# Q, K, V and router logits by token from one product per tile, turned by VectorE and transposed back, in a new written order

## The chip, the cores and the metric

The kernel runs on one core of a Trainium2 chip. The metric is the device time of one execution in microseconds (us). The core's engines work side by side, each through its own list of instructions in order: TensorE (matmuls, in the profile PE, its weight loads PEld), VectorE (DVE), ScalarE (ACT), GpSimd (POOL), and SyncE (SP), which issues most transfers. They wait for one another through semaphores.

## The reference, cut to what matters

`x` has 16 items of 256 tokens with 128 numbers each, all float32. An attention layer with 16 heads of 8 numbers, then a layer of eight experts of which each token uses two; each layer is added to its input and normalized.

```python
qkv = (x @ w_qkv).reshape(B, S, 3, heads, head_dim)
Q, K, V = qkv[:, :, 0], qkv[:, :, 1], qkv[:, :, 2]
Q, K = apply_rope(Q), apply_rope(K)      # x * cos + concat([-x2, x1]) * sin, halves of 4 numbers
attn = einsum('bqhd,bkhd->bhqk', Q, K) * head_dim ** -0.5
attn = softmax(where(causal, attn, NEG_INF))
x = layernorm(x + einsum('bhqk,bkhd->bqhd', attn, V).reshape(B, S, dim) @ w_proj + b_proj)
logits = flat_x @ W_router + b_router    # the two largest choose the experts and weigh them
out = layernorm(x + sum over the two chosen e of w_e * (relu(x @ W1[e] + b1[e]) @ W2[e] + b2[e]))
```

## The kernel before

`main_path` registers its work as some 1,550 small operations in a plan: each has an engine, a function that issues its instructions, and the operations that it waits for. `Plan.order` then issues them in one list, `ORDER`, written out by hand as the numbers under which they were registered. On each engine the instructions run in the order of that list. Costs and ranks given to `op` don't enter in the version that runs; only `ORDER` does.

`attention(b)` handles one item of 256 tokens. Two transposes (L780) turn `x` so that its 128 numbers lie along the partitions, and ScalarE copies the result to `xT` (L783). For Q and then K, `project` (L793) makes two products of 128 x 256: with the weights `wqk_sb`, and with `wsw_sb`, the same weights with the halves of each head exchanged (four copies at the start, L651). `turn_parts` multiplies these by the cosine and sine tables in `rope_sb` (L802, L803), and a sum gives the turned Q or K with the head's numbers along the partitions, in `qk` (L810). ScalarE makes four copies of Q, `qTm`, each with all heads but a quarter masked to zero (L822). V and the part of the router's logits that depends on `x` come from a third product by token (`project_v`, L838, 136 columns for each half of the tokens); `place_v` copies V into the padded `va` and the logits next to `x` (L847, L851).

Scores are made in three rounds (L871), each into the one buffer `sc`; ScalarE takes the exponential (L896), and GpSimd sets to zero what the causal mask forbids (L881). `weigh` (L912) multiplies with V. The sums of the exponentials go through memory and come back spread over partitions; VectorE multiplies by their inverse (L956), `project_o` (L966) makes the attention's result, and VectorE adds `x`, takes the moments and normalizes (L978 to L996).

Tokens of four, four and two items, and then of six, are routed (`route`): VectorE computes logits (L1077 to L1080), chooses (L1067 to L1090) and counts places, and GpSimd scatters the rows into memory (L1140). An expert block reads up to 256 such rows, and does the two layers (L1339, L1360) with ScalarE's bias and relu between them (L1352); GpSimd sends the rows back (L1387). The blocks of the first ten items follow the attention of the last ones in the list. At the end `combine` adds and normalizes; `keep_warm` gives TensorE a few products to do meanwhile (L1557).

The buffers named `m` are three buffers of TensorE's result memory, shared by transposes, projections, routing counts and blocks.

Of the kernel before, what the change touches and what calls it, by code (L numbers as in the profile page):

```python
# [11 lines left out]
F32 = mybir.dt.float32  # L12
# [299 lines left out]
7 0 45 46 1 14 47 9 15 12 2 11 50 29 81 6 3 4 22 10 13 48 49 5 82 51 52 24 56 54 53 86 17 21 19  # L312
23 87 30 57 93 55 59 94 16 58 88 18 60 20 25 83 121 65 31 61 26 157 84 85 122 123 124 91 66 89
68 158 44 90 62 92 63 159 160 161 126 32 95 96 125 127 197 128 162 133 132 64 163 131 98 69 99
67 198 70 71 8 97 130 72 33 101 104 129 102 100 164 233 169 103 234 134 73 74 141 75 142 166
105 106 107 108 135 143 167 136 27 109 76 170 202 203 204 168 28 110 138 165 139 199 111 137
144 209 656 200 201 140 208 112 171 145 206 146 147 172 655 77 148 177 173 149 113 178 78 150
179 151 238 79 210 239 207 174 152 34 205 80 175 114 653 176 235 180 658 115 116 236 211 237
117 118 240 212 181 182 183 184 185 153 186 35 244 245 214 243 215 187 188 213 273 120 119 220
154 657 217 216 242 155 274 246 278 279 659 275 276 241 218 250 219 280 251 277 221 309 310 281  # L320
284 189 222 223 247 282 190 248 311 156 252 224 249 191 192 193 253 37 285 225 256 314 283 254
286 312 290 194 195 196 664 313 291 226 255 315 316 257 385 386 665 258 662 227 259 260 261 293
666 36 390 391 392 318 317 294 319 320 667 672 670 287 262 671 228 288 654 387 668 295 263 349
321 292 322 669 388 389 289 350 326 678 296 297 298 327 264 680 229 673 395 323 324 328 679 299
300 265 301 394 354 355 351 352 329 302 353 230 356 325 231 393 232 332 303 396 330 405 661 333
406 38 674 675 676 331 357 266 267 358 360 399 334 335 400 336 425 677 41 268 361 304 397 337
338 339 426 340 407 402 398 362 359 401 427 537 681 403 686 269 430 538 366 408 305 367 428 429
431 404 409 410 432 434 685 270 363 435 688 364 411 271 306 682 436 433 542 369 341 307 412 413
# [126 lines left out]
def main_path(  # L455
# [87 lines left out]
    def load_x(b):  # L543
# [5 lines left out]
        )  # L549

    load_x(0)
    qk_op = dma(
        -99.0, 128, lambda: load(wqk_sb, w_qkv[:, 0 : 2 * D].rearrange("d (s e) -> d s e", s=2))
    )
    rope_op = [
# [1119 lines left out]
```

## Time and profile before

Three runs took 426.84 us at the median, 424.04 and 431.35 at the ends. The profile is of one other execution, which took 373.53 us.

| | us |
|---|---|
| profiled execution | 373.53 |
| its span, first to last instruction | 372.1 |
| first exponential starts, last one starts | 12.7, 185.5 |
| TensorE busy with L793, L838 | 42.5, 10.4 |
| VectorE busy with L802, L803, L810 | 40.0 |
| ScalarE busy with L896, L822, L847 | 90.1, 29.6, 5.9 |

Busy times of matmuls overlap[...]: 128 instructions of L793 sum to 42.5 us, though the engine starts one every 0.215 us. So a matmul's price is read from the time until the next one can start, and busy time is used only to compare stages. "Idle before" in a group is time in which the engine had nothing to do just ahead of these instructions, with the instruction that ended it.

### The profile page before, as it was taken

Reading aid. Unit: us, or ns where it says so; the run is one execution under the profiler, and the core shown is the slowest. Engines: PE = TensorE matmul, PEld = TensorE weight load, DVE = VectorE, ACT = ScalarE, POOL = GpSimd, SP = SyncE. Lnnn points to the kernel's source line nnn. Section 1 sums busy time; section 2 is a strip of 40 time slices with the busy share of each in tenths; the row PEclk is TensorE's granted clock in tenths of the full one; section 3 lists DMA queues with packets and bytes.
Section 4 is the critical chain, followed back from the end, with each engine's and each line's share of the span. In section 5 each row is a group of like instructions: output and inputs, shape, how many; then the busy total and the mean of one; then the engine's idle time right before and its main releaser. Section 6 shows DMA issues by size and latency. Waiting matters only on the chain.

```text
span 372.1 us, 9773 instructions
## 1 busy us (share of the span) xinstructions
PE 332.6 (89%) x2960; PEld 246.6 (66%) x2960; DVE 202.6 (54%) x731; ACT 252.3 (68%) x547; POOL 218.0 (59%) x252
## 2 busy tenths in 40 slices
PE   5999999979999696797999887999999899989980
PEld 3554555545566353444589767999898899989960
DVE  3440566786368879854567872143321267635551
ACT  2889778878788665677655453666666489978642
POOL 5155343446887489488822567777777446553632
PEclk9999999999999999699999999899999999999997
DMA  4100354131321221165345436665765687776472
GB/s 127 44 3 13 113 75 118 32 102 62 118 63 55 74 59 40 31 154 171 87 114 152 132 93 170 162 187 155 218 196 156 178 249 237 231 204 194 142 213 76
DMA packets 53098, 46.51 MB, mean 125 GB/s; under 512 B 14610, under 2 KB 39577, under 8 KB 53042
## 3 DMA queue, kind: packets, MB, share of 16 engines
q1 hardware_dynamic: 48626, 37.36, 37.5%
q0 software_dynamic: 4416, 8.47, 6.8%
q8 instruction: 27, 0.44, 0.5%
q14 instruction: 29, 0.24, 0.2%
HBM read 33.53 MB, written 12.67 MB: 124 GB/s over the span
## 4 chain that ended last, share of the span: by engine, by line
PE 55%; DVE 16%; ACT 11%; DMA 6%; issue 5%; POOL 4%; ACTq 0%; DVEq 0%; POOLq 0%; SPq 0%
PE m L1339 14%; PE m L1360 13%; PE sc L871 8%; PE ps_o L912 7%; ACT pr L896 7%; PE m L793 4%; PE m L966 3%; POOL rows L1140 2%; DMA rows_in<-rows 2%; DVE lg L1079 2%; DVE x_sb L996 2%; POOL pr L881 2%; PE ps_o L1557 1%; DMA out_dram<-yout 1%; PE m L1323 1%
## 5 line engine op out<-in xcount | busy, mean ns | idle before, releaser
L896 ACT ACTIVATE pr<-sc 128x2048 f32<-128x2048 f32 x48 | 90.1, 1877 | 26.8 <-PE sc L871 24.9
L1387 POOL DMA_INDIRECT back<-y,rows_in x74 | 72.8, 984 | 57.0 <-ACT y L1379 33.8
L881 POOL TENSOR_SCALAR_AFFINE_SELECT pr<-pr 128x1024 f32<-128x1024 f32 (+1 forms) x48 | 67.3, 1412 | 58.8 <-ACT pr L896 58.5
L1352 ACT ACTIVATE hT<-m,b_sb 128x128 f32<-128x128 f32 (+1 forms) x224 | 71.7, 407 | 21.8 <-PE m L1339 19.1
L1140 POOL DMA_INDIRECT rows<-x_sb,dest x64 | 65.3, 1020 | 22.7 <-issue 17.0
L1360 PE MATMUL m<-w_sb,hT 128*128 x592 | 75.5, 277 | 2.0 <-issue 1.1
L1339 PE MATMUL m<-rT,w 128*128 128x128 f32 (+1 forms) x448 | 75.8, 315 | 1.0 <-DVE rT L1332 0.4
L1360 PEld LDWEIGHTS m<-w_sb,hT 128*128 128x128 f32 x592 | 70.9, 192 | 4.8 <-ACT hT L1352 1.7
L1339 PEld LDWEIGHTS m<-rT,w 128*128 128x128 f32 x448 | 63.0, 194 | 5.9 <-DVE rT L1332 1.1
L871 PE MATMUL sc<-qTm,qk 32*128 32x512 f32 x384 | 55.7, 650 | 6.6 <-ACT pr L896 5.0
L912 PE MATMUL ps_o<-pr,va 128*32 128x128 f32 (+1 forms) x1024 | 49.9, 334 | 2.5 <-POOL pr L881 2.4
L1379 ACT ACTIVATE y<-y,rows_in 128x128 f32<-128x128 f32 x74 | 27.7, 401 | 30.4 <-DVE y L1370 30.1
L912 PEld LDWEIGHTS ps_o<-pr,va 128*32 128x32 f32 x1024 | 28.3, 111 | 29.4 <-issue 12.9
L1370 DVE TENSOR_TENSOR y<-m,b_sb 128x128 f32<-128x128 f32 (+1 forms) x56 | 18.7, 334 | 51.1 <-PE m L1360 41.8
L822 ACT ACTIVATE qTm<-qk,rows_sb 128x256 f32<-128x256 f32 x64 | 29.6, 506 | 1.8 <-DVE qk L810 1.8
L871 PEld LDWEIGHTS sc<-qTm,qk 32*128 32x128 f32 x384 | 15.2, 185 | 19.3 <-ACT pr L896 12.2
L793 PE MATMUL m<-xT,wqk_sb 128*128 128x256 f32 x64 | 22.5, 436 | 0.9 <-ACT xT L783 0.9
L802 DVE TENSOR_TENSOR part<-m,rope_sb 128x256 f32<-128x256 f32 x32 | 13.1, 410 | 18.6 <-PE m L793 18.1
L966 PEld LDWEIGHTS m<-wproj_sb,o 128*128 128x128 f32 x128 | 16.1, 190 | 7.2 <-issue 1.9
L956 DVE TENSOR_TENSOR o<-o,spread 128x512 f32<-128x512 f32 x16 | 13.7, 853 | 12.2 <-DMA spread<-recs 12.2
L793 PE MATMUL m<-xT,wsw_sb 128*128 128x256 f32 x64 | 20.0, 395 | 0.0
L1332 DVE COPY rT<-m 128x128 f32<-128x128 f32 (+1 forms) x32 | 10.6, 340 | 16.1 <-PE m L1323 14.2
(152 smaller groups left out, 362.6 us busy)
## 6 DMA issues: line engine op xcount, KB each, us to landing
w<-in_L_ffn_W_dram SPq DMA_DIRECT2D x56, 256.0 KB
spread<-recs SPq DMA_DIRECT2D x16, 256.0 KB
ys<-back SPq DMA_DIRECT2D x16, 256.0 KB
rows_in<-rows SPq DMA_DIRECT2D x38, 65.0 KB
rows_in<-rows SPq DMA_DIRECT2D x18, 130.0 KB
x<-in_L_attn_x_dram SPq DMA_DIRECT2D x16, 128.0 KB
w_sb<-in_L_ffn_W_dram SPq DMA_DIRECT2D x8, 256.0 KB
out_dram<-yout SPq DMA_DIRECT2D x16, 128.0 KB
```

Of the source, the lines that this page charges most:

```text
L793: nc.tensor.matmul(ps.get()[:, c, :], w[:, s, :], xT.get(), start=True, stop=True)
L822: lambda j=j: nc.scalar.activation(qTm.get()[:, j, :], qk.get()[:, 0], AF.Copy, scale=rows_sb[:, j : j + 1]),
L871: nc.tensor.matmul(ps.get()[:, g], qk.get()[rg, 1, ts(kt, P)], qTm.get()[rg, js, kt * P : S], start=True, stop=True,)
L881: nc.gpsimd.affine_select(out=pr.get()[:, :, :, 0:P], in_=pr.get()[:, :, :, 0:P], compare_op=ALU.is_ge, fill=0.0, base=0, pattern=[[0, GRO ...
L896: lambda pr=pr, ps=ps: nc.scalar.activation(pr.get(), ps.get(), AF.Exp),
L912: nc.tensor.matmul(pso.get()[ts(g, 32), t, kt * P : S], va_t[:, kt, 2 * g + t].rearrange("p u c -> p (u c)")[:, 16 * u : 16 * u + 32], pr. ...
L1140: nc.gpsimd.indirect_dma_start(out=g.rows[:, :], out_offset=bass.IndirectOffsetOnAxis(ap=g.dest[:, k, t - g.t0 : t - g.t0 + 1], axis=0), i ...
L1339: nc.tensor.matmul(ps_h[i].get()[:, c, :], w.get()[:, ts(i * per + c, P)], rT.get()[:, 0 : n * P], start=True, stop=True,)
L1352: nc.scalar.activation(hT.get()[:, at, 0 : n * P], ps_h[i].get()[:, c, :], AF.Relu, bias=bias)
L1360: nc.tensor.matmul(ps_y.get()[:, i, :], hT.get()[:, c, i * P : (i + 1) * P], w2_sb[:, bass.ds(e, 1), c, :].rearrange("p o d -> p (o d)"), ...
L1379: nc.scalar.activation(y.get()[:, i, :], y.get()[:, i, :], AF.Copy, scale=rows_in.get()[:, i, D + 1 : DX],)
L1387: put = nc.gpsimd.indirect_dma_start(out=g.back[:, :], out_offset=bass.IndirectOffsetOnAxis(ap=rows_in.get()[:, i, D : D + 1].bitcast(I32) ...
```

## The change

Q, K, V and the logits of half an item's tokens (128) now come from one product: `xT` of these tokens against all 392 columns of `w_sb`, so that tokens lie along the partitions. VectorE turns Q and K there, with tables by token: two short products take each half of the heads times the sine into `side` (the halves exchanged by the way the operand is read), one product in place takes the cosine, and one sum writes `turned`. `place_v` copies V and the logits out of the same buffer, once per half of the tokens. Four transposes (`turn_heads`) put the heads back along the partitions, into one buffer `ps_t`: VectorE copies K out of it as `kT`, and ScalarE's four masks read Q from it directly. The scores then read `kT` and `qTm`.

The second set of weights with its copies and the two large tables are gone. 16 KB of the table are loaded (`waves`) and transposed once at the start; the scale of Q goes into the mask's factors. `keep_warm` takes another operand. `ORDER` is a new list throughout: the sequence of items, blocks and scatters in it differs too.

```diff
 ORDER = """
-7 0 45 46 1 14 47 9 15 12 2 11 50 29 81 6 3 4 22 10 13 48 49 5 82 51 52 24 56 54 53 86 17 21 19
...
+5 0 44 45 3 13 1 2 49 14 50 9 7 8 30 156 51 46 47 52 157 4 12 48 57 55 54 56 53 10 6 161 29 162
...
-    wqk_sb = const.tile([P, 2, D], F32, name="wqk_sb")
-    wvr_sb = const.tile([P, DR], F32, name="wvr_sb")
-    rope_sb = const.tile([P, 2, 2, S], F32, name="rope_sb")
+
+    w_sb = const.tile([P, 3 * D + E], F32, name="w_sb")
+    wr_sb = w_sb[:, 3 * D : 3 * D + E]
+
+    waves = const.tile([HD, 2, S], F32, name="waves")
+    turns_sb = const.tile([P, NT, 2, HD], F32, name="turns_sb")
...
-    qk_op = dma(
-        -99.0, 128, lambda: load(wqk_sb, w_qkv[:, 0 : 2 * D].rearrange("d (s e) -> d s e", s=2))
+    w_ops = [
+        dma(-99.0, 192, lambda: load(w_sb[:, 0 : 3 * D], w_qkv)),
+        dma(-96.0, 4, lambda: load(wr_sb, w_router)),
+    ]
+    waves_op = dma(
+        -98.0,
+        16,
+        lambda: load(waves, rope.rearrange("p (a c s) -> p a c s", a=2, c=2)[0:HD, 1]),
     )
-    rope_op = [
-        dma(
-            -98.0,
-            256,
-            lambda s=s: load(
-                rope_sb[:, :, s, :],
-                rope.rearrange("p (a c s) -> p a c s", a=2, c=2)[:, s],
-            ),
-        )
-        for s in range(2)
-    ]
     rows_op = dma(-97.0, 2, lambda: load(rows_sb, rows))
-    vr_ops = [
-        dma(-96.0, 64, lambda: load(wvr_sb[:, 0:D], w_qkv[:, 2 * D : 3 * D])),
-        dma(-96.0, 4, lambda: load(wvr_sb[:, D:DR], w_router)),
-    ]
 
...
-    wsw_sb = const.tile([P, 2, D], F32, name="wsw_sb")
-    swap_ops = []
-    for s in range(2):
-
-        def swap_halves(s=s):
-            src = wqk_sb[:, s, :].rearrange("p (h t i) -> p h t i", t=2, i=HD // 2)
-            dst = wsw_sb[:, s, :].rearrange("p (h t i) -> p h t i", t=2, i=HD // 2)
-            for t in range(2):
-                V.tensor_copy(dst[:, :, t, :], src[:, :, 1 - t, :])
-
-        swap_ops.append(op("DVE", 0.6, -90.0 + s, swap_halves, after=[qk_op]))
+    rows_op = op(
+        "DVE",
+        0.1,
+        -92.0,
+        lambda: V.tensor_scalar(rows_sb, rows_sb, HD**-0.5, None, ALU.mult),
+        after=[rows_op],
+    )
+    ps_r = tile_of(ps_m, "m", [P, NT, 2, HD])
+
+    def turn_waves():
+        for t in range(NT):
+            for c in range(2):
+                nc.tensor.transpose(
+                    ps_r.get()[:, t, c, :], waves[:, c, ts(t, P)], ident[0:HD, 0:HD]
+                )
+
+    mats(-95.0, 0.5, turn_waves, writes=[ps_r], after=[waves_op, ident_op])
+    turns_op = op("DVE", 0.16, -95.0, lambda: V.tensor_copy(turns_sb, ps_r.get()), reads=[ps_r])
...
-        qk = tile_of(p3, "qk", [P, 2, S])
-        qTm = tile_of(p2, "qTm", [P, 4, S])
-        for s in range(2):
-            ps, part = tile_of(ps_m, "m", [P, 2, S]), tile_of(p2, "part", [P, S])
-
-            def project(s=s, ps=ps):
-                for c, w in enumerate((wqk_sb, wsw_sb)):
-                    nc.tensor.matmul(
-                        ps.get()[:, c, :], w[:, s, :], xT.get(), start=True, stop=True
+
+        va = tile_of(p1, f"va{b % len(vaug)}", [])
+        va.get = lambda: va_t
+        turned, side = tile_of(p2, "turned", [P, NT, 2 * D]), tile_of(p2, "side", [P, NT, 2 * D])
+        for t in range(NT):
+            ps = tile_of(ps_m, "m", [P, 3 * D + E])
+
+            def project(t=t, ps=ps):
+                nc.tensor.matmul(
+                    ps.get(), xT.get()[:, ts(t, P)], w_sb, start=True, stop=True
+                )
+
+            def turn_parts(t=t, ps=ps):
+                def by_head(v):
+                    return v.rearrange("p (h u i) -> p h u i", u=2, i=HD // 2)
+
+                def table(c):
+                    w = turns_sb[:, t, c, :].rearrange("p (o u i) -> p o u i", o=1, u=2)
+                    return w.to_broadcast([P, 2 * HEADS, 2, HD // 2])
+
+                both = ps.get()[:, 0 : 2 * D]
+                q, o = by_head(both), by_head(side.get()[:, t, :])
+                for u in range(2):
+                    V.tensor_tensor(
+                        o[:, :, u, :], q[:, :, 1 - u, :], table(1)[:, :, u, :], ALU.mult
                     )
-
-            mats(z, 0.96, project, reads=[xT], writes=[ps], after=[swap_ops[s]])
-
-
-
-            def turn_parts(s=s, ps=ps, part=part):
-                V.tensor_tensor(part.get(), ps.get()[:, 0], rope_sb[:, 0, s, :], ALU.mult)
-                V.tensor_tensor(ps.get()[:, 1], ps.get()[:, 1], rope_sb[:, 1, s, :], ALU.mult)
-
-            op("DVE", 0.76, z, turn_parts, reads=[ps], writes=[ps, part], after=[rope_op[s]])
+                V.tensor_tensor(q, q, table(0), ALU.mult)
+                V.tensor_tensor(turned.get()[:, t, :], both, side.get()[:, t, :], ALU.add)
+
+            def place_v(t=t, ps=ps):
+                nc.scalar.copy(
+                    va_t[:, t].rearrange("p w u c -> p (w u) c")[:, :, 0:HD],
+                    ps.get()[:, 2 * D : 3 * D].rearrange("p (h d) -> p h d", d=HD),
+                )
+                nc.scalar.copy(xt.get()[:, t, D:DR], ps.get()[:, 3 * D : 3 * D + E])
+
+            mats(z, 0.68, project, reads=[xT], writes=[ps], after=w_ops)
             op(
                 "DVE",
-                0.38,
+                1.3,
                 z,
-                lambda s=s, ps=ps, part=part: V.tensor_tensor(
-                    qk.get()[:, s], ps.get()[:, 1], part.get(), ALU.add
-                ),
-                reads=[ps, part],
-                writes=[qk],
+                turn_parts,
+                reads=[ps],
+                writes=[ps, turned, side],
+                after=[turns_op],
                 part="turn",
             )
+            op(
+                "ACT",
+                0.3,
+                z,
+                place_v,
+                reads=[ps],
+                writes=[va, xt],
+                after=[va_ops[b % len(vaug)]],
+                part="place",
+            )
+        ps_t, kT = tile_of(ps_m, "m", [P, 2, S]), tile_of(p3, "kT", [P, S])
+        qTm = tile_of(p2, "qTm", [P, 4, S])
+
+        def turn_heads():
+            for s in range(2):
+                for t in range(NT):
+                    nc.tensor.transpose(
+                        ps_t.get()[:, s, ts(t, P)], turned.get()[:, t, ts(s, D)], ident
+                    )
+
+        mats(z, 0.46, turn_heads, reads=[turned], writes=[ps_t])
+        op(
+            "DVE",
+            0.34,
+            z,
+            lambda: V.tensor_copy(kT.get(), ps_t.get()[:, 1]),
+            reads=[ps_t],
+            writes=[kT],
+        )
         for j in range(4):
             op(
                 "ACT",
                 0.4,
                 z,
                 lambda j=j: nc.scalar.activation(
-                    qTm.get()[:, j, :], qk.get()[:, 0], AF.Copy, scale=rows_sb[:, j : j + 1]
+                    qTm.get()[:, j, :], ps_t.get()[:, 0], AF.Copy, scale=rows_sb[:, j : j + 1]
                 ),
-                reads=[qk],
+                reads=[ps_t],
...
-        va = tile_of(p1, f"va{b % len(vaug)}", [])
-        va.get = lambda: va_t
-        ps_v = tile_of(ps_m, "m", [P, NT, DR])
-
-        def project_v():
-            for t in range(NT):
-                nc.tensor.matmul(
-                    ps_v.get()[:, t, :],
-                    xT.get()[:, ts(t, P)],
-                    wvr_sb,
-                    start=True,
-                    stop=True,
-                )
-
-        def place_v():
-            nc.scalar.copy(
-                va_t.rearrange("p t w u c -> p t (w u) c")[:, :, :, 0:HD],
-                ps_v.get()[:, :, 0:D].rearrange("p t (h d) -> p t h d", d=HD),
-            )
-            nc.scalar.copy(xt.get()[:, :, D:DR], ps_v.get()[:, :, D:DR])
-
-        mats(z, 0.56, project_v, reads=[xT], writes=[ps_v], after=vr_ops)
-        op("ACT", 0.33, z, place_v, reads=[ps_v], writes=[va, xt], after=[va_ops[b % len(vaug)]])
...
-                        qk.get()[rg, 1, ts(kt, P)],
+                        kT.get()[rg, ts(kt, P)],
...
-                idle.get()[:, 0, :], ident, rope_sb[:, 0, 0, :], start=True, stop=True
+                idle.get()[:, 0, :], ident, w_sb[:, 0:S], start=True, stop=True
```

## Prediction

> **What bounds the kernel now.** First the page's totals and a table by stage: each row is a stretch in us, its length, then busy time and instructions of TensorE (matmul, weight load), VectorE, ScalarE and GpSimd.
>
> ```profile
> PE 332.6 (89%) x2960; PEld 246.6 (66%) x2960; DVE 202.6 (54%) x731; ACT 252.3 (68%) x547; POOL 218.0 (59%) x252
> ```
>
> ```profile
> 12.00:187.00 175.00, 158.10 (x1688) 88.51 (x1681) 109.63 (x359) 133.75 (x184) 108.58 (x97) 0.98 0.28 73
> 187.00:350.00 163.00, 154.51 (x1198) 143.26 (x1198) 78.84 (x311) 106.56 (x336) 97.24 (x101) 0.99 0.63 179
> ```
>
> The reader is to see two stages. The edit lies in the first, attention; the second, the expert blocks, is TensorE nearly alone. Next, the chain of waits (start, us, what) says what the attention stage is made of:
>
> ```profile
> 21.07 1.19 PE sc L871 x8
> 22.28 1.89 ACT pr L896
> 24.21 1.19 PE sc L871 x8
> 25.42 1.88 ACT pr L896
> ...
> 40.87 1.11 PE sc L871 x8
> 42.07 1.89 ACT pr L896
> ```
>
> There is one score tile `sc`: scores (L871) wait for the exponential (L896) of the round before, which waits for its scores. A round takes 3.15 us (21.07 to 24.21), of which 1.2 leave ScalarE free and 2.0 leave TensorE free. 48 such rounds are 151 us; the exponentials run from 12.7 to 187.4, so 24 us are lost to rounds that took longer. The chain over a later window gives the price of what the change touches:
>
> ```profile
> 100.13 0.37 PE m L780 x2
> 100.50 0.93 PE m L838 x8
> 101.43 1.07 PE sc L871 x8
> 102.50 1.06 PE m L793 x4
> 103.56 0.22 PE m L780 x2
> 103.78 0.86 PE m L793 x4
> ```
>
> L793 is one `project` (two products of 256 columns), 0.86 us when the next follows it; L838 is V of two items, 0.93; L780 two transposes, 0.22. Adding up all chain pieces up to 205 us, L793 has 14.3 us and L838 3.2: 17.5 us of the path. The stage issues 16 x (1.72 + 0.46) = 34.9 us of them, so about half of this work is on the path and half lies under exponentials. The three turn lines of VectorE (L802, L803, L810) have 7.2 us of 40 there, 18%. Last, the groups (busy us, mean ns of one, idle before):
>
> ```profile
> L802 DVE TENSOR_TENSOR part<-m,rope_sb 128x256 f32<-128x256 f32 x32 | 13.1, 410 | 18.6 <-PE m L793 18.1 <-DMA wproj_sb<-in_L_attn_w_proj_dram 0.4
> L803 DVE TENSOR_TENSOR m<-m,rope_sb 128x256 f32<-128x256 f32 x32 | 13.8, 433 | 2.0
> L810 DVE TENSOR_TENSOR qk<-m,part 128x256 f32<-128x256 f32 x32 | 13.1, 420 | 0.8
> L1370 DVE TENSOR_TENSOR y<-m,b_sb 128x128 f32<-128x128 f32 x38 | 11.1, 292 | 27.9 <-PE m L1360 21.5 <-DMA back<-y,rows_in 2.4 <-issue 1.6
> L847 ACT COPY va<-m 128x256 f32<-128x256 f32 x16 | 5.9, 373 | 2.3 <-PE m L838 2.2
> L1079 DVE TENSOR_TENSOR lg<-lg,rstd_sb 128x32 f32<-128x32 f32 x1 | 4.6, 4626 | 0.0
> ```
>
> VectorE often waits for L793 (18.1 us): it has room on average, but not everywhere. L1079 shows one small operation taking 4.6 us, and what stands behind it on VectorE waits as long.
>
> [...] L803 stays at 433 ns, while L1079 (two SBUF inputs) took 4626. All new turning operations read PSUM and one SBUF operand, so I cost them without that stretch. [...] The new code gives VectorE and ScalarE the same tile twice (turn and `place_v`; `kT` and the masks), so I take these as done in turn; no row of before shows such a pair.
>
> **The change, part by part.**
>
> 1. *TensorE.* Out: 1.72 + 0.46 = 2.18 us per item. In: two products of 392 columns, each 0.43 x 392/256 = 0.66, and four transposes, 0.44: 1.76. Saved 0.42 x 16 = 6.7 us. By the chain's half this is 3.4 us off the path. Against it stands the new order: adding these prices between successive scores in the written lists, and letting each round last at least 3.15 us, the 47 rounds come to 155 us before and 157 after, because the lighter work is spread less evenly (some rounds have none, others 3.7 us). I take the middle of -3.4 and +2: **-0.7**, bounds -6.7 and +4.
> 2. *VectorE.* Out: 2 x (410 + 433 + 420) = 2.53 us per item. In, per half of the sequence: two products of 128 elements (292 each, the nearest row), one of 256 in place (433), one sum (420), so 1.44; twice, and the `kT` copy (425, as the 128x256 `rT` copies from PSUM at L1332): 3.30. More by 0.77 x 16 = 12.3 us; the four swap copies (0.5 us) go. On the path 18%: **+2.1**. Lower bound 0, if the stage's idle VectorE time takes it all. The runs of four elements and the repeated table aren't in the trace; if all of them ran at half rate, the four short products would cost 0.13 us more each and the two in-place ones 0.27 (1 ns per element, from 292 against 424 ns at L1370), 1.07 per item, 17 us, another 3 on the path.
> 3. *ScalarE.* V is placed in two parts: 128 elements are 100 ns less than 256 (L1352: 375 against 475), so 0.27 + 0.19 (L851), twice 0.92 against 0.56: 5.8 us more. The masks (L822, 506 ns) now read PSUM, where L1352 has 475: 64 x 0.03 = 2 us less. ScalarE's pieces are 31 us of the stage's chain, of 134 busy, 23%: **+0.8**. Bounds: -1.5 if a mask falls to L847's 373 ns, +1.3.
> 4. *Waits.* A score now stands behind product, turning, a second visit to TensorE, then masks and `kT` in turn. TensorE works in order: if VectorE is late, `turn_heads` holds the projections, weighings and scores behind it. The tile `ps_t` is kept until the masks are done, which stand among exponentials of 1.88 us, and the same three `m` buffers serve everything. Two more crossings per item, 0.1 us each (idle times of 0.2 and more stand before many first loads), half on the path: **+1.6**. Bounds 0 and 16, the latter at 1 us per item.
> 5. *Start and end.* `rope` (512 KB in two transfers) is out, 16 KB of it in, one transfer of 192 KB for 128 + 64: two issues of 0.45 us less on SyncE's queue before `x` of the next items. The first exponential started at 12.70. Now xT as before at 4.34; the products 1.4 each (at first eight L793 took 3.78 us, half rate), to 7.2; the second turning 8.7; transposes 9.2; four masks in 1.7; `kT` 0.45; scores 1.2; 0.4 for crossings: 13.0. **+0.3**, bounds -1 and +1.5. At the end `missing` (0.5 us) stands before the last `shift`, which waits for GpSimd's 0.9 us anyway: 0; 0.5 if that cover is gone.
> 6. *Blocks and routing.* Same instructions, another order; TensorE is busy 155 of 163 us, so nothing on average: **0**, bounds -4 and +4.
>
> Sum: -0.7 + 2.1 + 0.8 + 1.6 + 0.3 = **+4.1 us** on the profiled execution's 373.5 (span 372.1 and 1.4 around it): 377.6, 1.1%. The median of the runs shown is 426.84, 53 us above that execution, and no view shows where these lie. Added as it stands or by ratio (x 1.14, 4.7) the step gives **431 us**.
>
> **The cases.** The three runs shown spread over 1.7%, so about 2% is what a measurement tells from no change.
>
> - *A, likeliest (0.44): the saving is given back.* Score and exponential still alternate; 377.6, that is 431, own range 424 to 438. For it: half of the removed work lay hidden, and the order leaves rounds uneven.
> - *B (0.23): TensorE is the bound, and the saving counts whole.* If the runs' extra 53 us are slower matmuls, 6.7 x 1.14 = 7.7 us go, and an order that loses 3 us less makes 416. For it: 158 of 175 us busy. Against: the 24.9 us in which ScalarE waited for scores and the chain's even share for both.
> - *C (0.30): VectorE becomes the late engine.* In the routing stretches (by the stage table's finer cut, VectorE is busy 16 to 18 of 20 us between 120 and 160) turning stands behind choices and stalls like L1079's, and TensorE waits at `turn_heads`. At 1 us per item 16 us: 447. It decides from 0.55 us per item (8.5 us, 2%).
> - *D (0.03): it doesn't do what it says*, for example turning at half rate throughout with everything on the path: 450 and more.
>
> Range 413 to 450: B and most of C. Faster by over 2% (under 418.3): most of B and a little of A, 0.23. Slower by over 2% (above 435.4): C, D and a tail of A, 0.39. Within: 0.38.
>
> **What would show it.** Right: TensorE's busy time some 7 us less, VectorE's some 12 more, exponentials still 3.15 us apart at best and their last end near 190. B: the last exponential ends by 181. C: new rows in which TensorE's weight loads at `turn_heads` or the scores wait for VectorE, over 8 us in all. Wrong altogether: short products well above 0.3 us, or a block stage whose length moves by more than 4 us.

## The result, and the profile after

The changed kernel took 449.98 us at the median (447.87 to 453.10), the kernel before 427.06 beside it: a ratio of 1.057, with a 95% interval of 1.046 to 1.067. It is slower; 431 was predicted.

The 53 us between the profiled execution of before and its other runs turned out to belong to the chip: on one chip the kernel before takes 373 us, on the others used 424 to 430. The first profile of the changed kernel (span 446.7 us) is from a chip of the second kind and can't be laid beside that of before. Both kernels were run again on the chip with 373 (e1 and e4 below), and unless another run is named the lines that follow are from this pair. There the ratio is 1.047 (1.036 to 1.058), 18 us between the medians, and the spans of the profiled executions are 370.8 and 391.1 us.

The page's totals of the kernel before (e1), then of the changed kernel (e4):

```profile
PE 331.7 (89%) x2960; PEld 245.4 (66%) x2960; DVE 201.8 (54%) x731; ACT 252.2 (68%) x547; POOL 216.7 (58%) x252
PE 337.4 (86%) x2900; PEld 236.5 (60%) x2900; DVE 215.2 (55%) x777; ACT 252.4 (65%) x579; POOL 216.2 (55%) x252
```

VectorE is 13.4 us busier. TensorE's busy time didn't fall: the lines of the changed products and transposes did, from 52.6 us (L793, L838) to 40.9 (L795, L850), but lines that didn't change took longer at a lower granted clock (0.942 of full speed over the span, 0.986 before), the scores 59.7 in place of 55.7. In the table by stage (columns as in the prediction, the number before the last two is the granted clock) the first row is the attention stage of the changed kernel, the second its expert blocks:

```profile
14.00:204.00 190.00, 160.19 (x1603) 78.18 (x1604) 121.79 (x389) 132.57 (x208) 108.80 (x124) 0.91 0.23 67
207.00:370.00 163.00, 154.26 (x1183) 143.03 (x1176) 77.97 (x316) 106.84 (x337) 95.80 (x100) 0.98 0.63 180
```

The blocks take as long as before; attention has grown from 175 to 190 us, at a clock of 0.91 in place of 0.98. What one line's instructions took, and when the first and the last started, dates it: the exponential, then the weights of the blocks' first layer, in the kernel before,

```profile
L896 ACT ACTIVATE pr<-sc x48: 1856/1877/1895, 12.2 to 184.3; 128x2048 f32<-128x2048 f32 x48
L1339 PEld LDWEIGHTS m<-rT,w x448: 186/192/245, 185.5 to 346.4; 128*128 128x128 f32 x150
```

and in the changed kernel:

```profile
L917 ACT ACTIVATE pr<-sc x48: 1858/1877/1938, 13.8 to 202.1; 128x2048 f32<-128x2048 f32 x48
L1360 PEld LDWEIGHTS m<-rT,w x448: 186/192/337, 207.5 to 366.6; 128*128 128x128 f32 x150
```

The first exponential starts 1.6 us later, the last one 17.8 later, the blocks 22.0 later; they last 159.1 us in place of 160.9. The intervals between the 48 exponentials, added up, say in which rounds the time went:

| intervals | before (e1) | changed (e4) | old way, new list (e2) |
|---|---|---|---|
| the first 19 | 64.3 | 64.8 | 65.9 |
| 20 and 21 | 7.8 | 12.4 | 11.0 |
| 22 to 31 | 35.3 | 36.5 | 35.9 |
| 32 to 47 | 64.7 | 74.6 | 67.2 |
| sum | 172.1 | 188.3 | 180.0 |

The first 19 are level. The loss lies at 79 to 91 us and from 128 us on, where routing shares VectorE with the turning. The new instructions themselves cost what was said (groups: busy us, mean ns of one, idle before):

```profile
L868 ACT ACTIVATE qTm<-m,rows_sb 128x256 f32<-128x256 f32 x64 | 27.6, 482 | 11.0 <-DVE kT L859 9.2 <-PE m L850 1.6
L810 DVE TENSOR_TENSOR side<-m,turns_sb 128x128 f32<-128x128 f32 x64 | 15.3, 280 | 13.8 <-PE m L795 13.8
L813 DVE TENSOR_TENSOR m<-m,turns_sb 128x256 f32<-128x256 f32 x32 | 13.8, 432 | 1.8
L814 DVE TENSOR_TENSOR turned<-m,side 128x256 f32<-128x256 f32 x32 | 13.6, 424 | 1.1
L817 ACT COPY va<-m 128x128 f32<-128x128 f32 x32 | 8.5, 278 | 8.8 <-DVE turned L814 7.6 <-DVE rows_sb L641 1.2
L859 DVE COPY kT<-m 128x256 f32<-128x256 f32 x16 | 6.6, 414 | 22.2 <-ACT qTm L868 22.2
```

These VectorE rows add up to 49.3 us, where the three turning lines of before had 40.0. So 9.3 of the 13.4 us are the new turning and the keys' copy; the rest is the balance of old operations that took longer or shorter, the normalizing (L1017), for one, 16.0 in place of 11.5.

The last row is new in kind: for 22.2 us VectorE had nothing to do because the keys' copy, at the head of its queue, waited for ScalarE to finish masks out of the same bank. The first row has the mirror image: masks waited 9.2 us for the keys' copy. What that means in one place, VectorE's timeline of e4 at intervals 20 and 21 (start, us, then the operation):

```profile
74.40 2.03 DVE L1017 TENSOR_SCALAR x_sb<-x_sb,mv_sb,rstd_sb 128x128 f32<-128x128 f32 x1
76.35 0.21 DVE L1098 TENSOR_TENSOR off<-mv_sb,cs_sb 128x64 f32<-128x64 f32 x1
...
81.99 0.16 DVE L1111 TENSOR_TENSOR d<-m,m 128x8 f32<-128x8 f32 x1
82.06 0.48 DVE L810 TENSOR_TENSOR side<-m,turns_sb 128x128 f32<-128x128 f32 x2
...
84.44 0.42 DVE L814 TENSOR_TENSOR turned<-m,side 128x256 f32<-128x256 f32 x1
...
87.15 2.02 DVE L1131 TENSOR_TENSOR hot<-hot,place 128x64 f32<-128x64 f32 x1
89.21 0.22 DVE L1133 TENSOR_REDUCE dest<-hot 128x8 int32<-128x64 f32 x1
89.34 0.42 DVE L859 COPY kT<-m 128x256 f32<-128x256 f32 x1
```

Logits and choice run from 76.35 to 82.1 before the turning of item 7 gets its 2.8 us; then come the counts and places, and only at 89.34 the keys' copy, for which a score waits on TensorE:

```profile
89.81 1.14 PE L892 MATMUL sc<-qTm,kT 32*128 32x512 f32 x8 [0.21 <-DVE kT L859]
```

In e1 the turnings stand between parts of the same routing work, and no second visit follows:

```profile
73.27 0.42 DVE L810 TENSOR_TENSOR qk<-m,part 128x256 f32<-128x256 f32 x1
...
74.72 0.42 DVE L810 TENSOR_TENSOR qk<-m,part 128x256 f32<-128x256 f32 x1
75.06 0.21 DVE L1067 TENSOR_REDUCE m<-lg 128x8 f32<-128x64 f32 x1
...
79.16 0.42 DVE L810 TENSOR_TENSOR qk<-m,part 128x256 f32<-128x256 f32 x1
79.50 1.02 DVE L1102 COPY starts<-begin 128x8 f32<-128x8 f32 x1
```

### The profile page after: what moved, and what is told of

Its sections match the earlier page's. It is cut to its first block, busy times and chain, and to the rows that moved or that the text cites. A ratio compares the mean times of both kernels' runs of the same rounds, so it can differ in the third digit from the quotient of the medians.

```text
span 446.7 us, 9748 instructions
## 1 busy us (share of the span) xinstructions
PE 363.0 (81%) x2900; PEld 251.0 (56%) x2900; DVE 212.1 (47%) x777; ACT 252.2 (56%) x579; POOL 216.1 (48%) x252
## 4 chain that ended last, share of the span: by engine, by line
PE 49%; DVE 15%; ACT 15%; another core or an unknown queue 9%; issue 6%; SPq 2%; DMA 2%; POOL 1%; ACTq 0%; DVEq 0%
PE m L1360 14%; PE m L1381 13%; ACT pr L917 9%; PE sc L892 7%; PE ps_o L933 4%; PE m L987 3%; ACT qTm L868 3%; DVE x_sb L1017 2%; PE m L795 2%; PE m L1344 2%; PE ps_o L1578 1%; ACT hT L1373 1%; DVE key L1089 1%; DVE m L813 1%
## 5 line engine op out<-in xcount | busy, mean ns | idle before, releaser
L1408 POOL DMA_INDIRECT back<-y,rows_in x74 | 73.1, 988 | 100.0 <-ACT y L1400 65.9
L1360 PE MATMUL m<-rT,w 128*128 128x128 f32 (+1 forms) x448 | 82.5, 332 | 5.1 <-issue 3.3
L1381 PE MATMUL m<-w_sb,hT 128*128 x592 | 80.2, 287 | 6.2 <-ACT hT L1373 2.5
L892 PE MATMUL sc<-qTm,kT 32*128 32x512 f32 x384 | 63.4, 687 | 20.9 <-ACT pr L917 15.7
L1360 PEld LDWEIGHTS m<-rT,w 128*128 128x128 f32 x448 | 67.5, 208 | 12.1 <-issue 4.8
L1400 ACT ACTIVATE y<-y,rows_in 128x128 f32<-128x128 f32 x74 | 27.3, 402 | 28.2 <-DVE y L1391 24.7
L892 PEld LDWEIGHTS sc<-qTm,kT 32*128 32x128 f32 x384 | 17.2, 193 | 43.3 <-ACT pr L917 27.4
L868 ACT ACTIVATE qTm<-m,rows_sb 128x256 f32<-128x256 f32 x64 | 27.7, 487 | 9.1 <-DVE kT L859 8.2
L795 PE MATMUL m<-w_sb,xT 128*128 128x392 f32 x64 | 31.3, 600 | 1.7 <-issue 1.0
L1344 PE MATMUL m<-ident,rows_in 128*128 128x128 f32 x45 | 12.3, 327 | 18.3 <-ACT hT L1373 7.3
L1353 DVE COPY rT<-m 128x128 f32<-128x128 f32 (+1 forms) x32 | 10.8, 341 | 24.7 <-remote 10.7
L987 PE MATMUL m<-wproj_sb,o 128*128 128x136 f32 x128 | 21.6, 318 | 0.6 <-ACT qTm L868 0.6
L810 DVE TENSOR_TENSOR side<-m,turns_sb 128x128 f32<-128x128 f32 x64 | 15.2, 279 | 12.2 <-PE m L795 12.2
```

Source lines behind the costliest of these rows:

```text
L795: nc.tensor.matmul(ps.get(), xT.get()[:, ts(t, P)], w_sb, start=True, stop=True)
L868: lambda j=j: nc.scalar.activation(qTm.get()[:, j, :], ps_t.get()[:, 0], AF.Copy, scale=rows_sb[:, j : j + 1]),
L892: nc.tensor.matmul(ps.get()[:, g], kT.get()[rg, ts(kt, P)], qTm.get()[rg, js, kt * P : S], start=True, stop=True,)
L987: nc.tensor.matmul(ps_p.get()[:, q, :], o.get()[:, t, ts(q, P)], wproj_sb[:, t, :], start=(t == 0), stop=(t == 1),)
L1360: nc.tensor.matmul(ps_h[i].get()[:, c, :], w.get()[:, ts(i * per + c, P)], rT.get()[:, 0 : n * P], start=True, stop=True,)
L1381: nc.tensor.matmul(ps_y.get()[:, i, :], hT.get()[:, c, i * P : (i + 1) * P], w2_sb[:, bass.ds(e, 1), c, :].rearrange("p o d -> p (o d)"), ...
```

## The experiments

**Whether it is the data's way or the list.** Four kernels on the chip with 373: both kernels as they are; the old way of the data issued in the new list (e2); and the new way in the old list (e3), each as far as dependences and buffers let an operation stand at its place. The first line of the lists, e2:

```diff
-7 0 45 46 1 14 47 9 15 12 2 11 50 29 81 6 3 4 22 10 13 48 49 5 82 51 52 24 56 54 53 86 17 21 19
+7 0 45 46 2 3 1 5 6 14 15 50 51 52 11 9 10 31 157 47 48 49 57 58 158 4 56 54 53 55 12 8 162 30 163
```

and e3:

```diff
-5 0 44 45 3 13 1 2 49 14 50 9 7 8 30 156 51 46 47 52 157 4 12 48 57 55 54 56 53 10 6 161 29 162
+5 0 44 45 1 7 10 3 13 14 9 28 80 2 46 49 4 12 21 8 11 47 48 81 50 51 52 53 23 57 55 54 85 16 20 18
```

> The kernel before, unchanged, once more, for a profile of an execution that lasts as long as its timed runs (427 us; the profile shown took 373). If the 53 us between them are a lower TensorE clock all along, the new profile shows a span near 425 with a granted clock near 0.85 and the same stages stretched evenly; if they are stalls, it shows pieces in which TensorE issues nothing for microseconds, in both stages, as the profile of the changed kernel has (407 us of its span in attention and blocks, 40 us longer than before in the block stage that the edit doesn't touch). If the profile again takes some 373 us, the time around it is not to be seen in a profile.

> The kernel before with its own products and turning, issued in the changed kernel's list (each operation at the place of its counterpart, V just before the old place of the transposes). Theory 'list': the new list alone makes it slower, 440 to 450 us, ratio 1.03 to 1.05. Theory 'flow': it stays within 2% of before, 420 to 435, since the handoffs between product, turning and transposes are absent. Both in part: in between, near 437.

> The changed kernel's products, turning and transposes, issued in the old list as far as its waits and buffers allow (some operations move by up to 60 places, because the product's buffer is kept until V is placed). Theory 'flow': slower than before by as much as the changed kernel or more, 445 to 465 us. Theory 'list': near before, 425 to 435. A list not made for it may cost on its own, so only a time near before is clear evidence.

> The changed kernel once more, on the same chip as the others: 440 to 455 us. If its block stage again lasts some 200 us in the profile where the first profile of before had 163, the stalls there belong to it in every execution; if the stage varies by tens of us between its two profiles, they come and go.

Measured, as ratios to before: e2 1.034 (1.022 to 1.046), e3 1.179 (1.163 to 1.195), e4 1.047 (1.036 to 1.058); medians of e1 to e4 373.81, 384.72, 441.95 and 391.02 us. The expected times were meant for a chip with 427, so only the ratios can be held against them: e2 lies where theory 'list' had it, e3 far beyond both of its ranges. The new list costs 10 us between the spans (370.8 and 381.2), 12 between the medians, with the old way of the data in it, and the table above shows 3.2 of its 7.9 us between exponentials in intervals 20 and 21 again. VectorE has the same instructions in e2 as in e1 and is still 7.6 us busier, since some of them took longer:

```profile
PE 332.3 (87%) x2960; PEld 244.9 (64%) x2960; DVE 209.4 (55%) x731; ACT 252.5 (66%) x547; POOL 215.6 (57%) x252
```

So the list's cost and that of VectorE's time are not cleanly apart. In the old list, on the other hand, the new way did far worse, though operations were moved by up to 60 places to let it run: VectorE's waits in e3 are led by the keys' copy,

```profile
DVE kT L858 <- PE m L849: 36.1, 15, 10.0
```

36.1 us in 15 waits, the longest 10.0. My reading, argued from these two runs: the longer way needs a list that starts it earlier, and such a list is worse for the rest.

**What VectorE's work costs.** e5 leaves most of the turning out, e8 does part of it twice; later e16 gave the kernel before more VectorE work in its own list. The edits in this order:

```diff
-                for u in range(2):
-                    V.tensor_tensor(
-                        o[:, :, u, :], q[:, :, 1 - u, :], table(1)[:, :, u, :], ALU.mult
-                    )
-                V.tensor_tensor(q, q, table(0), ALU.mult)
-                V.tensor_tensor(turned.get()[:, t, :], both, side.get()[:, t, :], ALU.add)
+                V.tensor_tensor(
+                    turned.get()[:, t, :].rearrange("p (h u i) -> p h u i", u=2, i=HD // 2),
+                    q,
+                    table(0),
+                    ALU.mult,
+                )
```

```diff
-                for u in range(2):
+                for u in (0, 1, 0, 1):
```

```diff
-                V.tensor_tensor(part.get(), ps.get()[:, 0], rope_sb[:, 0, s, :], ALU.mult)
+                for _ in range(2):
+                    V.tensor_tensor(part.get(), ps.get()[:, 0], rope_sb[:, 0, s, :], ALU.mult)
```

> The changed kernel, with the turning cut down: per tile VectorE makes one product, Q and K times the cosine table, straight from PSUM to SBUF; the two sine products and the sum are left out, so the output is not the reference's. That takes 2 x 0.28 + 0.42 = 0.98 us per tile off VectorE, 31 us over 32 tiles, and leaves the way of the data as it is: product, VectorE, transposes, kT on VectorE, masks on ScalarE, three buffers. Theory V (VectorE's time in the turning costs the 18 us): the kernel comes back to the time of the kernel before or below it, 362 to 376 us on the chip on which the kernel before took 373, and the rounds of 5 to 7 us between exponentials shrink to 4 to 5. Rival X (the longer way costs it: one more crossing to VectorE and back, a bank shared by VectorE and ScalarE, product buffers held longer): it stays at 384 to 391, ratio 1.03 to 1.05.

> The changed kernel with the two sine products of every tile issued twice (the second time writes the same values again): 64 x 0.28 = 17.9 us more on VectorE and nothing else. Theory V (VectorE's time in the attention stage is paid at about one for one in the routing stretches and partly elsewhere): 400 to 410 us on a chip with 391 for the changed kernel. Rival X (the way of the data and the buffers, VectorE itself having room): 391 to 396.

> The kernel before, in its own list, with the cosine product of Q and of K issued twice (the second writes the same values again): 32 x 0.42 = 13.4 us more on VectorE, as much as the change added (201.8 to 215.2), with no new wait between engines. If VectorE's time as such is the cost (theory V), 1.025 to 1.04 of the kernel before. If it is what the turning stands behind and what stands behind it, the second visit with the keys and the list made for it (theory P), 1.00 to 1.015.

> The changed kernel, unchanged, beside the two others: 1.045 to 1.06 of the kernel before, as twice so far.

All four ran on one chip, each beside the kernel before: e5 1.026 (1.020 to 1.031), e18, the changed kernel itself, 1.050 (1.045 to 1.055), e8 1.063 (1.056 to 1.070), e16 1.011 (1.007 to 1.015). VectorE's busy times are 183.9, 212.1, 224.6 us, and 209.7 in e16, against 199.0 in e11, a profile of before from another chip. (What is issued twice adds less busy time than twice its duration: two short products in a row take 0.48 us in the timeline above, not 2 x 0.28.) With 427 us for the kernel before on this chip, a busy microsecond of VectorE costs 10.3/28.2 = 0.37 us from e5 to e18, 5.7/12.5 = 0.46 from e18 to e8, and 4.7/10.7 = 0.44 in e16 (0.6 if e1's 201.8 is taken for 199.0). The three agree within their intervals (0.26 to 0.48, 0.18 to 0.73, 0.28 to 0.61), in both kernels and in both directions: some 0.4. The 9.3 to 13.4 us of busy time that the change added are then 4 to 5 us, about a quarter of the loss. Theory V, which put all of it there, falls in all three. Rival X came nearer: e8 is 1.013 of the changed kernel, at the upper edge of its range, but e5, under its 1.03, and e16 say that VectorE's work isn't free. In e16 theory P's range holds, and the place is the one seen before: intervals 20 and 21 take 11.2 us, where e11, before without the addition, has 7.8.

**The second visit.** e6 lets ScalarE copy the keys, ahead of the masks; e9 keeps the copy on VectorE but at the place in the list that e6 gave it.

```diff
         op(
-            "DVE",
+            "ACT",
             0.34,
             z,
-            lambda: V.tensor_copy(kT.get(), ps_t.get()[:, 1]),
+            lambda: nc.scalar.copy(kT.get(), ps_t.get()[:, 1]),
```

> The changed kernel, with the turned keys copied to SBUF by ScalarE, ahead of the four masks of the same item, in place of VectorE; everything else stands where it stood. VectorE loses 16 x 0.42 = 6.6 us and ScalarE gains about as much, and the bank with the transposed queries and keys has one reader only. Rival X (the hand-over of that bank between VectorE and ScalarE stalls both): the waits of masks for the keys' copy and of the keys' copy for masks go, 13 us of them in the window of 130 to 203 us of the changed kernel, and the time falls to 380 to 385 on a chip with 373 for the kernel before and 391 for the changed kernel. Theory V (VectorE's work as a whole, the turning above all): a fall by no more than 3 us, 388 to 392, since only a fifth of the added VectorE work goes. Rival S (ScalarE, in front of the exponentials, is the tightest engine): slower than the changed kernel, 393 to 398.

> The changed kernel with another list, nothing else: the copy of the turned keys, still VectorE's, comes in every item ahead of the four masks that read the same bank, as it did in the run with the keys by ScalarE. Theory H (the keys' copy stands on VectorE behind ScalarE's masks and holds up all of VectorE's queue: 22 to 39 us of such waits): the waits of the keys' copy for masks fall from some 25 us to under 3 us, and most of what the keys by ScalarE brought comes by the list alone: 440 to 445 on a chip with 430 for the kernel before and 449 for the changed kernel (0.98 to 0.99 of the changed kernel). Rival L (VectorE's load: it was the 6.6 us less on VectorE that helped): under 3 us, 446 to 451; the wait then reappears as the keys' copy waiting for TensorE's transposes and the masks waiting for the keys' copy.

e6: 1.030 (1.026 to 1.035), 8 us (5 to 11) less than e18 on the same chip, as rival X had it; VectorE's 7.1 us less explain 3 of them. e9: 1.059 (1.053 to 1.064), no gain, with the same list as e6. VectorE's waits ahead of the keys' copy in e18 and then in e9, and ScalarE's in e9, tell why:

```profile
DVE kT L859 <- ACT qTm L868: 28.7, 9, 9.4
```

```profile
DVE kT L857 <- PE m L848: 16.4, 10, 4.3
```

```profile
ACT qTm L866 <- DVE kT L857: 11.9, 6, 7.0
```

The copy's wait for the masks, 28.7 us in e18, is gone, as theory H had it, but the time didn't fall: ahead of the masks the copy waits for TensorE's transposes (16.4 us), and the masks wait for it (11.9, where e18 has 8.6). At either place in VectorE's queue something is held up; off the queue, ScalarE's extra 3.6 us of busy time (256.6 against 253.0) cost less than that. So rival L's forecast for e9 held, though its reason covers only the 3 us. I put the rest, 5 us, down to the visit to VectorE's queue. It could also be the bank that two engines share; against that speaks e13 below, where VectorE alone reads the bank, in the same list, and nothing is won.

**The turning ahead of the choice.** e7 moves item 7's products and turning ahead of the choice, and three copies of keys forward; e17 joins this to e6. In e7 only the list differs. The numbers 311 and 314 are item 7's two turnings and 316 its four transposes; they stood behind 251 to 291 and now stand ahead of 254:

```diff
-259 667 666 292 312 314 315 669 670 288 293 295 671 316 320 321 318 317 350 668 296 260 261 262
...
+118 311 314 663 664 665 251 286 316 254 659 226 227 287 256 320 321 318 319 317 257 258 291 259
```

> The changed kernel with another list: for the item whose turning stood behind a choice of experts (item 7) the products and the turning come ahead of the choice and the keys' copy ahead of the count and places; for items 11 and 13 the keys' copy alone comes ahead of the choice. No instruction is added or taken away. If case C holds as the prediction put it, turning and keys that stand behind choices, the two rounds of 6.0 and 6.4 us near 79 to 91 us shrink to 3.5 to 4.5, those near 128 and 160 us by 1 to 2 us, and the time falls by 6 to 10 us, to 381 to 385 on a chip with 391 for the changed kernel. If VectorE's time as such is what is short (theory V), the choice comes later instead, its followers with it, and the gain is under 3 us.

> The changed kernel with the keys copied by ScalarE ahead of the masks (alone 1.030 of the kernel before) and, for item 7, products and turning ahead of the choice (alone, with two keys' copies moved, 1.040). If the two cure different rounds (the keys those after 95 us, the turning those at 79 to 91 us), 1.015 to 1.025; if the same, 1.028 to 1.035. Nothing is left out; neither reading expects it below the kernel before.

e7: 1.040 (1.034 to 1.045); the two rounds took 5.6 and 7.0 us in place of 6.4 and 6.0, 12.6 us together where there were 12.4, so at this place nothing is won. e17: 1.032 (1.027 to 1.036), no better than e6, and again 8 us below e18, which ran beside it. The turning does stand behind the choice, as case C had it, but which of the two stands first makes no difference here. e7's gain over e18, 4 us, is less than the 6 to 10 named for case C, and whether it is real is left open, since the intervals touch.

**Both parts of VectorE's load, and before beside it.** e10 joins the edits of e5 and e6; e11 is the kernel before.

> Two edits together: the two sine products and the sum of every turning left out (so the output is not the reference's) and the keys copied by ScalarE ahead of the masks. Alone they took about 10 and 8 us off the changed kernel. If VectorE's turning and the hand-over of the bank are two separate costs that make up the loss, they add: 430 to 433 on a chip with 430 for the kernel before, ratio 1.00 to 1.01. If both cure the same stalls, or a third cost is left (product buffers held longer, the longer way through VectorE and back), it stays at 436 to 441, ratio 1.015 to 1.025.

> The kernel before, unchanged, for its stages on the chip that the other runs of this call are on: 428 to 432 if it is the chip with 430, and the last exponential of attention near 195 to 199 us, the block stage as long as in the changed kernel and its variants (196 us from the first to the last weight load of the second layer), so that the whole loss lies in attention.

e10: 1.018 (1.008 to 1.027). Against e18 VectorE's busy time falls by 37.5 us (to 174.6) and the time by 13.7. Alone the two edits brought 10.3 and 8.2; the sum would be 4.9 us more, but by the intervals that difference is uncertain by 5.4, so whether they add is not settled. VectorE is 24 us less busy than in the kernel before (e11), and the kernel is still slower. What remains is neither VectorE's work nor the keys' copy.

e11 is as expected: its last exponential starts at 198.5 us, and the blocks' first-layer weights last 197.4 us. In e18, on another chip of the slower kind, these are 216.7 and 198.3. There, too, the loss lies ahead of the blocks.

**The product buffers.** Added up in the trace from a tile's first matmul to its last reader, the three buffers `m` are held 272 us by the attention's work in e1 and 411 in e4: a product 7.3 us, of which 4.0 until it is turned, since V is copied out of it only when an older item has given up its V buffer. e12 has a third V buffer and copies V soon after the turning; e13 copies the turned Q and K to SBUF at once, so that the masks read SBUF; e14 does both; e15 joins e12 and e6. The cores of the edits (e12, then e13):

```diff
-        const.tile([P, NT, HW, 2, 32], F32, tag=f"va{i}", name=f"va{i}") for i in range(2)
+        const.tile([P, NT, HW, 2, 32], F32, tag=f"va{i}", name=f"va{i}") for i in range(3)
```

```diff
-            lambda: V.tensor_copy(kT.get(), ps_t.get()[:, 1]),
+            lambda: V.tensor_copy(qk.get(), ps_t.get()),
```

> The changed kernel with three V buffers in place of two, so that V and the logits of a tile can be copied soon after its turning (the copies stand up to 35 places earlier in the list); `side` shrinks to one tile to make room; the rest is as it was. Theory M (the three product buffers are held too long and TensorE's next products wait for them): the product is held 5 to 6 us in place of 7 to 8, and the time falls by 5 to 10 us, to 1.033 to 1.045 of the kernel before (changed kernel 1.057). Rival (buffers have room, VectorE's time and its hand-overs are the cost): 1.05 to 1.06.

> The changed kernel with the turned queries and keys copied to SBUF by one VectorE copy of 128x512 in place of the 128x256 copy of the keys; the masks read SBUF, as in the kernel before, and the bank of the transposes comes free after that copy. The copy comes ahead of the masks in the list. VectorE gains an estimated 16 x 0.25 = 4 us (from 0.42 for 256 elements and 0.19 for 32 elements of the same engine). Theory M: the heads are held some 2.5 us in place of 5.3, and the time falls by 5 to 8 us, to 1.037 to 1.045 of the kernel before. Rival (VectorE's time): 1.055 to 1.07, since VectorE only gets more to do; the run with the list alone moved stayed at 1.059.

> The third V buffer with the early copies of V, and the queries and keys copied at once, together. Theory M: buffer time near that of the kernel before (some 300 us), 1.015 to 1.03 of the kernel before. Rival: 1.05 to 1.065.

> The third V buffer with the early copies of V, and the keys copied by ScalarE ahead of the masks (alone 1.030 of the kernel before). Theory M: the two add, 1.005 to 1.02. Rival (what the keys by ScalarE freed is all that was short besides VectorE's turning): 1.025 to 1.035. Nothing is left out, so if this is under 1.0 it would be the better kernel.

Measured: e12 1.071 (1.054 to 1.087), e13 1.061 (1.046 to 1.076), e14 1.073 (1.053 to 1.093), e15 1.052 (1.039 to 1.066). Theory M falls: in e12 a product is held 5.8 us (8.1 in e18) and in e15 all tiles together 351 (448 in e18), and nothing is won; e15 is even 2% behind e6. Of the rivals' ranges only the one for e13 holds; e12, e14 and e15 came out slower still. ScalarE's waits in e12 show the price of the early copies:

```profile
ACT va L816 <- DVE turned L813: 21.2, 13, 4.3
```

ScalarE now waits for the turning ahead of its exponentials, 21.2 us in 13 waits, where e18 had 2.2 in two. A buffer that comes free early helps only if the list has something to put into it. No version tried beats the kernel before.

## Why the prediction was wrong

The likeliest case, A, had +4.1 us. On one chip it is +18 between the medians and +20.3 between the spans. By the prediction's own steps:

- *Step 1, TensorE and order (-0.7, bounds -6.7 and +4): failed, and the largest error.* The instructions were priced nearly right: a product is two instructions in the trace, each mostly 0.33 or 0.43 us ahead of the next, so 0.66, as used, is the best case. But the order was priced at +2 by TensorE's prices between scores alone. With the old instructions it costs 10 to 12 (e2), and such a sum of one engine's work can't see waits on the others. The sign "TensorE 7 us less busy" didn't come either: 337.4 against 331.7, at a mean granted clock of 0.942 against 0.986.
- *Step 2, VectorE (+2.1): work about right, share too small.* Short products took 280 ns (292 predicted), the in-place one 432 (433), the sum 424 (420), the copy 414 (425): by the prediction's own sum 11.5 us more, where it had 12.3. That the engine's whole busy time grew by 13.4, so near to 12.3, is in part chance, since old operations that took longer are in it. The share of 18% on the path was read off the kernel before as a mean over the stage. The price of more work is some 0.4: 4 to 5 us.
- *Step 3, ScalarE (+0.8): sizes right.* V and logits took 0.28 and 0.19 us, masks 482 ns. Its share of the path wasn't tried alone. The lower bound of -1.5 doesn't follow from its numbers: 64 masks at 373 ns save 8.5 us, less 5.8 and times 23% that is -0.6.
- *Step 4, waits (+1.6, bounds 0 and 16): mis-sized.* Two crossings at 0.1 us were the wrong price for a visit to a queue. That VectorE and ScalarE take the shared bank in turn was an estimate; in the first profile of the changed kernel none of the 16 copies of keys overlaps one of the 64 masks. Taking the keys' copy off VectorE gave 8 us, 5 of them beyond its work.
- *Step 5 (+0.3, bounds -1 and +1.5):* 1.6 at the start, just outside. *Step 6 (0):* the blocks last 1.8 us less, within its bounds; but 4.2 us more lie between the last exponential and the blocks.

Ten to 12 us for the list, 4 to 5 for VectorE's work and 5 for the second visit make 19 to 22, where 18 to 20 are to be explained. This is an account and not a proof: the three come from different chips and pairs, the 5 of the second visit are uncertain by 3, e2's own VectorE time overlaps with the second part, and e10 leaves open whether the last two add. By the medians, the way of the data in the new list (e4 against e2) costs 6 us rather than 10. How much of the list's cost any list must pay for the longer way, and how much a better list would save, stays open.

Of the rivals, B is out: the last exponential started at 202. C (447 forecast) had the time, the place and the sign: at TensorE the weights for `turn_heads` waited 5.3 us and those for scores 3.2 for VectorE in e4, just over the 8 named. That 449.98 falls just inside the range of 413 to 450 is owed to C too, and its 447 was in part luck: it was 1 us per item, set and not measured, and it had no cost of the list. Its mechanism, VectorE's load, was about a quarter of the matter, and moving the turning ahead of the choice (e7) brought little. Still, the reason given for C, VectorE busy 16 to 18 of 20 us in the routing stretches, was better evidence than the mean that the sum used.

## What to carry to other kernels

A share of the path that was measured for an engine's present work isn't the price of more work on it: cost an addition in the stretches where that engine is fullest, and test it by issuing twice an instruction whose second run only writes the same values again. In a written order, count the visits that an item pays to each queue, not only the microseconds; here one more visit in the middle of the chain cost about as much as all of the added arithmetic. When a change needs a new order, put the old instructions into it (or the new ones into the old) to see what the order itself costs.

## What was not expected of the hardware

*TensorE's clock fell where TensorE waited.* From 130 to 187 us the tables by stage have these rows, e1 and then e4:

```profile
130.00:187.00 57.00, 48.98 (x526) 27.66 (x521) 39.04 (x136) 38.46 (x50) 43.86 (x44) 0.94 0.33 90
```

```profile
130.00:187.00 57.00, 45.76 (x364) 20.87 (x360) 37.51 (x137) 32.03 (x50) 35.70 (x38) 0.78 0.21 62
```

A granted clock of 0.78 in place of 0.94, with TensorE busy 45.8 us in place of 49.0. In TensorE's timeline of e4 the scores, of 1.14 us in most rounds, take 2.09 soon after an idle stretch of 3.58 us:

```profile
134.93 0.69 PE L1117 MATMUL m<-hot,before 128*128 128x64 f32 x2 [3.58 <-ACT qTm L868]
...
136.69 2.09 PE L892 MATMUL sc<-qTm,kT 32*128 32x512 f32 x8 [0.65 <-ACT pr L917]
```

Whether such a stretch is what lowers the clock was not tried. In e4 the scores of one more round, at 82.77 us, took 1.82; in e1 those of a single round, at 153.44, took 2.09, and all scores together 4.0 us less (55.7 against 59.7). How much of the loss the clock makes wasn't separated.

*Stretches on VectorE.* The normalizing `L1017` has 342 ns at the median and took 2.03 us at 74.40. GpSimd's timeline has, at that moment,

```profile
74.30 2.05 POOL L902 TENSOR_SCALAR_AFFINE_SELECT pr<-pr 128x2048 f32<-128x2048 f32 x1 [1.13 <-ACT pr L917]
```

and another from 87.08 to 89.09, beside the 2.02 us of L1131. The prediction named an operation with two SBUF inputs (L1079), no `TENSOR_SCALAR`. Of the 32 normalizing operations two took over 1.2 us in the first profile of before (1.23 at 118.28 us, 2.03 at 187.48) and three in that of the changed kernel (2.04 at 74.13, 1.93 at 104.81, 2.04 at 128.55), each while such a GpSimd mask ran; what holds them up isn't in the trace.

*Chips differ by some 14%.* The kernel before takes 373.81 us at the median on one chip (e1) and 424 to 430 on the others used. Its first-layer weight loads run from 185.5 to 346.4 us in e1 and, on another chip, in e11:

```profile
L1339 PEld LDWEIGHTS m<-rT,w x448: 186/192/338, 199.7 to 397.1; 128*128 128x128 f32 x150
```

160.9 against 197.4 us for the same instructions of the same median duration. It shows in the waits: ahead of these weight loads TensorE's load side stood idle 2.4 us in e1 and 37.6 in e11. Why was not settled. Ratios between two kernels on one chip hardly depend on it (1.047, 1.050 and 1.057 for the changed kernel).
